# Fourth and fifth chunk of image 2 put off, and the first input sums of the next image's conv made during attention's last two units

## The chip, the core and the metric

The kernel runs on one core of a Trainium2 chip. A core has a matrix engine (TensorE, PE; PEld is its loading of weights), a vector engine (VectorE, DVE), a scalar engine (ScalarE, ACT), a third one for elementwise work (GpSimd, POOL) and queues that issue DMAs (SP and POOL among them). Engines run side by side, each in its own order, and wait for one another by semaphores. The metric is device time in microseconds (us), the median of several runs; a profile comes from one execution of its own.

## What is computed

Four images of 256 channels and 48x48 pixels go through two layers with residuals. Cut to what matters:

```python
for each layer: x = x + layer(group_norm(x))          # 32 groups

# layer 0
x = relu(batch_norm(conv3x3(x)))                      # fixed statistics
q, k, v = split(qkv_w @ x)                            # 8 heads of 32
out = v @ softmax(q.T @ k / sqrt(32)).T               # 2304 x 2304 per head
out = proj_w @ out + proj_b

# layer 1
guidance = conv3x3(x, W_cat)                          # 45 channels
outs = [x]
for i, d in enumerate((1, 6, 12, 24, 36)):
    w = softmax(guidance[:, 9*i : 9*i+9], axis=1)     # nine weights a pixel
    outs.append(sum(shift(x, dy*d, dx*d) * w[k] for k, (dy, dx) in ...))
y = W_scale @ concat(outs)                            # 1536 -> 256, a 1x1 conv
y = (y - mean(y)) / sqrt(var(y) + eps) * gamma + beta # over all four images
```

Everything is float32. The last line needs the statistics of y over all images, so nothing of the result is written before every y is known.

## The kernel before

**Stages.** The 256 channels are two halves of 128 partitions. An image's 2304 pixels are six chunks of 8 rows (384 pixels, `CH`). The stages in order: conv and q,k,v of image 0; attention 0; stage 1; attention 1; stage 2; attention 2; stage 3; attention 3; stage 4. Stage b (1 to 3) is one merged stretch: the second layer of image b-1 (`dynamic_filters`) and the conv and q,k,v of image b (`conv_blocks`) fill each other's waits. Stage 4 is the second layer of image 3 by itself, with what was put off, and then `finish`.

**Order of work.** The order on each engine is the order in which the program issues it. Within a merged stage a planner decides this: `clock` (class `Clock`) holds a modelled time for each engine, and a step adds its modelled duration. `drive(streams)` goes through a list of generators; each yields the modelled time at which its next step is due, and the first in the list that is due goes on. Where none is due, the next piece of the conv (`other`) is taken, if its own due time `need[0]` has come. `run(ns)` issues so much conv work by itself. Streams of stage b: `rest` (the conv's later input sums), `loads`, `far` (filters of dilation 6 to 36, as matmuls, in ACT and DVE copied to a tile `far`), `near` (dilation 1: nine times ACT copies a weight row `wb`, DVE multiplies it with the image into `prod`, L1792, and POOL adds `prod` into `near`, L1798), `filters` (guidance conv `pg`, softmax) and `mixes` (the 1x1 conv, `py`, chunk by chunk).

**Chunks put off.** `mixes` takes the chunks 0 to 5 in order. In stage 3 the chunks in `LATE` of image 2 aren't mixed: once their products are there, x (normalized), `near` and `far` are written to HBM, `late_d` (SP queue, L1864 and L1865: 384 KB and 1.5 MB). During attention 3 they come back, the first entry of `LATE` into the unused one of the two padded images `pads`; `late()` mixes them in stage 4 (matmuls `pl`), where they fill waits of image 3. `last_loads` loads the y of the other chunks from `y_d` in stage 4. For a chunk that is mixed, `done` copies y out of the accumulator (for chunk 5 into rows of the padded image, L1831), takes its statistics on DVE, and writes it to `y_d`.

**Memory.** Tiles are taken from pools. The pools of an attention reuse the memory of the stage before it and the other way round; the tile framework makes an instruction wait until what was there has been read or written.

**Attention.** Units 0 to 7 are 512 columns of queries for four heads (one of the halves); unit 8, `last`, is the last 256 columns of both halves. Each unit goes through 18 tiles of 128 keys, index m. `scores` makes four matmuls of 512 columns into PSUM (`so`, `se`) and two exponentials on ACT (L1330, L1331) into p, 128x2048; p has four buffers. `weigh` follows one step behind: matmuls `num` with v, and on DVE `acc` += p (L1370) for the softmax's denominator. At five values of m (`LENT`; four in the last unit) DVE adds only a quarter of p, and a DMA issued by POOL (L1372, L1374) adds the rest in memory, into a part of `ring`; at the unit's end DVE adds that to `acc`. `close(u)`, a unit or two later, sums `acc` over the partitions by matmuls (`den`, L1386), transposes, takes the reciprocal and scales the result `ao` on DVE. In the last unit the tiles m = 16 and 17 aren't added by DVE but go into `den` by matmuls, and `close` follows at once. `project` (matmuls `pp`, L1444) puts a chunk through proj_w, and DVE adds bias and residual into the padded image (L1453) and takes statistics (L655); five chunks are done at m = 6 of the units 3, 5, 7 (two) and 8, the sixth after attention. With each of the five a fifth of the next image is normalized by ACT (`spare`, `pieces`).

**The conv of images 1 to 3** (class `Blocks`) is a fast convolution with six input transforms along the rows: v1 to v4 are sums of rows of the normalized padded image d0 to d5 with factors 2 and 4, v0 and v5 likewise. They take one buffer each of 128x1200 (two halves of 600). `stage0` makes the first of them: two multiplications on ACT (L1013, L1014), ten sums on POOL (L1006); `along(i)` then takes differences along the columns (four POOL sums of 128x576, L1084), which are the moving operands of the matmuls `pc` (L1166; 128x288). `stage0` is called by `following[0]` when the last attention step has been issued, into the buffers of k and q. Tile order is v1, v2, v3, v4, v0, v5, each for two output halves `o` and four j. ACT and DVE combine the `pc` results into `one`, `two`, `held` and outputs `y`, to which ACT applies batch norm and ReLU (`relu`). `either` gives a sum to POOL or DVE by the planner's clock.

**The group norm between the layers.** `Norm.finish`: two aggregations on DVE, a matmul `pm` with the group matrix, squares on ACT, a matmul `pv`, and the reciprocal root; `shift_of` makes -mean*rstd on DVE (L685). Then DVE normalizes one half of the image and ACT the other, in two parts.

The start of a merged stage, after the last attention step:

```python
            while chunk < NCK:
                ...
                project(b, chunk, ao, pp, norm)
                chunk += 1
            table(AF.Sqrt)
            run(2400)
            for at, _ in enumerate(norm.finish(misc)):
                run((600, 700)[at])
            norm.shift_of()
```

Of the kernel before, what the change touches and what calls it, by code (L numbers as in the profile page):

```python
# [16 lines left out]
N = HH * WW  # L17
# [20 lines left out]
LATE = (5, 4)  # L38
# [19 lines left out]
def conv_preact_kernel(  # L58
# [487 lines left out]
    with tc.tile_pool(name="w", bufs=1) as wpool, tc.tile_pool(  # L546
# [98 lines left out]
        class Norm:  # L645
# [11 lines left out]
            def finish(self, psum_tile):  # L657

                mean = small.tile([P, NH], F32, tag=f"gmean{self.tag}", name=f"gmean_{self.name}", bufs=1)
                rstd = small.tile([P, NH], F32, tag=f"grstd{self.tag}", name=f"grstd_{self.name}", bufs=1)  # L660
                d2 = small.tile([P, NH], F32, tag="gd2", name=f"gd2_{self.name}")
                mv = self.mv
                for h in range(NH):
                    nc.vector.bn_aggr(mv[:, h, :], self.st[:, h].rearrange("p c s -> p (c s)"))
                yield
                pm = psum_tile(f"pm_{self.name}")
                nc.tensor.matmul(pm[:, :NH], gmat, mv[:, :, 0], start=True, stop=True)
                nc.scalar.copy(mean, pm[:, :NH])
# [82 lines left out]

        XT = WW // 2
# [222 lines left out]
        class Blocks:  # L975


            def __init__(self, b, gn):
                self.b = b
                self.d = [gn[:, :, r : r + HH - 3 : 4, :] for r in range(6)]  # L980
                k_, q, v = (
                    act.tile([P, NH * N], F32, tag=tag, name=f"cv_{b}_{tag}") for tag in "kqv"
                )
                at = NH * 2 * TJ * PADW
                v_ = [t[:, at * j : at * (j + 1)] for t in (k_, q) for j in range(3)]
                self.spare = [
                    t[:, at // 2 * j : at // 2 * j + 2 * TN]
                    for t, n in ((k_, 6), (q, 2)) for j in range(n)
                ]
                self.first = [t[:, 3 * at : 3 * at + 2 * TN] for t in (k_, q)]  # L990
                self.v = {
                    i: t.rearrange("p (h t w) -> p h t w", h=NH, w=PADW)
                    for i, t in zip((1, 2, 3, 4, 0, 5), v_)
                }
                z = 4 * NH * XN
                self.v[6] = v[:, z : z + at].rearrange("p (h t w) -> p h t w", h=NH, w=PADW)
                self.held = v.rearrange("p (j o n) -> p j o n", j=4, o=NH)
                self.of = {1: v[:, :z]}
                pad = gn.rearrange("p h r w -> p (h r w)")
                self.pad = [pad[:, z * j : z * (j + 1)] for j in range(2)]  # L1000
                self.end = {}
                self.passed = set()

# [55 lines left out]
            def axpy(self, out, x, a, y):  # L1059
                if len(x.shape) == 4:  # L1060
                    for h in range(NH):
                        self.axpy(out[:, h], x[:, h], a, y[:, h])
                    return
# [25 lines left out]
        def either(out, a, c, op, *after):  # L1089

            part = 0.5 if len(out.shape) == 2 and out.shape[-1] == XN else 1.0
# [6 lines left out]
        def conv_blocks(b, psum_tile, blocks, pool, hid):  # L1098
# [3 lines left out]
            rows = hid.rearrange("p h (t r w) -> p h t r w", r=4, w=WW)  # L1102
# [10 lines left out]
            def relus(limit):  # L1113
                while results and results[0][3] + 150 <= limit:
                    o, r, y, end = results.pop(0)
                    nc.scalar.activation(
                        rows[:, o, :, r, :], rows_of(y), AF.Relu,
# [39 lines left out]
            for t, (i, o) in enumerate(TILES):  # L1157
                u = us.pop(t)
                y = target(i, o).rearrange("p (n s) -> p n s", s=2)
                for n, j in enumerate((1, 2, 0, 3)):  # L1160
# [33 lines left out]
                    else:  # L1194
                        to = y[:, :, n - 2]
                        if busy_dve():
                            nc.scalar.mul(to, m, 1.0 if j == 0 else -1.0)
                            end = clock("ACT", 450, clock.t["PE"])
                            either(to, to, two[:, n - 2], ALU.add, end)
                        else:  # L1200
                            if j == 0:
                                tt(to, m, two[:, 0], ALU.add)
                            else:
                                tt(to, two[:, 1], m, ALU.subtract)
                            end = clock("DVE", 480, clock.t["PE"])
                        if n == 3:
                            after(i, o, y.rearrange("p n s -> p (n s)"))
# [87 lines left out]
        def attention(b, q, k_, vT, pools, spare, project, scratch, following):  # L1295
# [41 lines left out]
            def weigh(u, m, p):  # L1337
# [6 lines left out]
                several = len(units[u]) > 1  # L1344
# [68 lines left out]
            for i, (u, m) in enumerate(steps):  # L1413
# [18 lines left out]
            assert not spare  # L1432
# [30 lines left out]
        def dynamic_filters(b, ao, chunk, norm, other, pools):  # L1463
# [482 lines left out]
            def last_loads():  # L1946
# [5 lines left out]
                for c in range(NCK - len(LATE)):  # L1952
                    tag, bufs = ("prod", PRODS) if c < PRODS else ("cat1", 2)
# [34 lines left out]
            if not alone:  # L1988
                clock.t["POOL"] = clock.t["PE"] + 12500
# [12 lines left out]
            run(2400)  # L2002
            for at, _ in enumerate(norm.finish(misc)):
                run((600, 700)[at])
            norm.shift_of()
            for part in range(2):
# [9 lines left out]
                run((900, 1600)[part])  # L2016
# [7 lines left out]
            else:  # L2024
                streams.insert(0, coming[-1].rest() if coming else iter(()))
# [120 lines left out]
        for b in range(B + 1):  # L2146
# [170 lines left out]
            spare = []  # L2317
            following = [lambda: None] * 2
            clear(pads[b % 2] if b else pads[1])
            if b + 1 < B:  # L2320
# [19 lines left out]
                spare = [lambda some=todo[i::5], f=pieces: f(some) for i in range(5)]  # L2340
            norm1 = Norm("n1", b)
            q, k_, vT = qkv[b]
            with tc.tile_pool(name=f"work0_{b}", bufs=2) as work0, tc.tile_pool(
# [4 lines left out]
                    lambda c, ao, pp, b=b, n=norm1: project(b, c, ao, pp, n), scratch, following,  # L2348
                )
# [75 lines left out]
```

## Time and profile before

| what | us |
|---|---|
| runs | 2758.36, 2760.39, 2761.98; median 2760.39 |
| the profiled execution, its own time | 2758.79 |
| its span, first to last instruction | 2756.9 |
| conv and q,k,v of image 0 | 151.5 |
| attention 0, 1 | 364.70, 369.95 |
| stage 1, 2 | 294.65, 295.67 |
| stage 4 | 257.26 |

Busy over the whole span: PE 94%, DVE 76%, ACT 66%, POOL 29%; the mean granted clock of TensorE is 0.982 of full speed. The lines below name an instruction by its line (L1370), engine, operation, output and inputs. "128x2048" is partitions by elements. A number after x is a count. In brackets stands how long the engine was idle before the instruction, and what ended that. Stage borders are taken where attention's first matmuls start and where its last scores end; a few instructions of the neighbour lie on either side.

### The profile page before, as it was taken

What the parts mean: (1) busy time and instruction counts of PE and PEld (TensorE: products, weight loads), DVE (VectorE), ACT (ScalarE), POOL (GpSimd) and SP (SyncE); (2) the same over time, 40 slices, a digit from 0 to 9 for tenths busy, and PEclk for the clock granted to TensorE, in tenths of its full rate; (3) what the DMA queues carried; (4) which work ended last, traced back from release to release, by engine and by line L of the source; (5) the groups of instructions that cost most, each with busy time, mean ns of one, the idle gap of its engine ahead of it and who ended that gap; (6) DMA issues with size and microseconds to landing.
All of it is one profiled execution on the core that took longest, in us unless ns stands there. A gap on an engine that the chain in (4) does not pass through costs nothing. (4 is left out here: it accounts for less than half of the span.)

```text
span 2756.9 us, 42411 instructions
## 1 busy us (share of the span) xinstructions
PE 2602.5 (94%) x16906; PEld 1097.9 (40%) x16906; DVE 2090.5 (76%) x2030; ACT 1807.9 (66%) x2251; POOL 790.0 (29%) x871
## 2 busy tenths in 40 slices
PE   6999999999999999989999999998997999999994
PEld 5632222455552222445554222244554222235452
DVE  7778888657749888857765898884875988885476
ACT  3478988634458888844346888873344988874344
POOL 5100100466520100167560100026644000100462
PEclk9999999999999999999999999999998999999997
DMA  4704544322252444422224444442225334432365
GB/s 177 215 20 97 112 98 101 81 78 82 77 102 58 109 98 92 110 75 77 81 64 83 97 101 102 104 92 72 76 66 140 99 91 99 104 81 74 108 194 180
DMA packets 135982, 273.67 MB, mean 99 GB/s; under 512 B 56040, under 2 KB 97936, under 8 KB 134880
## 3 DMA queue, kind: packets, MB, share of 16 engines
q0 software_dynamic: 25952, 135.74, 21.5%
q1 hardware_dynamic: 109824, 135.14, 18.3%
q8 instruction: 135, 2.21, 0.3%
q14 instruction: 71, 0.58, 0.1%
HBM read 112.12 MB, written 36.04 MB: 54 GB/s over the span
## 5 line engine op out<-in xcount | busy, mean ns | idle before, releaser
L1370 DVE TENSOR_TENSOR acc<-acc,p 128x2048 f32<-128x2048 f32 (+1 forms) x568 | 1052.0, 1852 | 122.5 <-ACT p L1331 72.6
L1331 ACT ACTIVATE p<-se 128x1536 f32<-128x1536 f32 x648 | 938.6, 1449 | 0.0
L1322 PE MATMUL so<-q,k 32*128 32x512 f32 (+1 forms) x1440 | 728.2, 593 | 27.3 <-ACT p L1330 27.1
L1322 PE MATMUL se<-q,k 32*128 32x512 f32 (+1 forms) x4320 | 737.6, 593 | 4.6 <-DVE prod L1792 4.6
L1351 PE MATMUL num<-p,vT 128*32 128x512 f32 (+1 forms) x5760 | 709.1, 561 | 2.2 <-ACT ao L1380 2.2
L1330 ACT ACTIVATE p<-so 128x512 f32<-128x512 f32 x648 | 388.4, 599 | 205.6 <-PE se L1322 87.7
L1798 POOL TENSOR_TENSOR near<-near,prod 128x384 f32<-128x384 f32 x384 | 389.5, 1045 | 344.7 <-DVE prod L1792 342.9
L1322 PEld LDWEIGHTS so<-q,k 32*128 32x128 f32 x1440 | 216.7, 183 | 545.2 <-ACT p L1330 504.1
L1374 POOL DMA_DIRECT2D ring<-p x124 | 105.5, 851 | 777.9 <-ACT p L1331 464.6
L1351 PEld LDWEIGHTS num<-p,vT 128*32 128x32 f32 x5760 | 135.7, 108 | 479.1 <-issue 448.1
L1792 DVE TENSOR_TENSOR prod<-wb,pad 128x768 f32<-128x768 f32 x192 | 181.8, 953 | 102.4 <-ACT wb L1779 71.8
L1893 PE MATMUL py<-far,wsc 128*128 128x384 f32 x704 | 236.0, 488 | 0.0
L1322 PEld LDWEIGHTS se<-q,k 32*128 32x128 f32 x4320 | 227.5, 183 | 10.4 <-issue 5.5
L1779 ACT COPY wb<-ws 128x384 f32<-128x384 f32 x216 | 109.2, 509 | 147.3 <-DVE prod L1792 103.2
L1372 POOL DMA_DIRECT2D ring<-p x32 | 17.9, 559 | 610.6 <-ACT p L1331 451.3
L1494 ACT COPY far<-far 128x512 f32<-128x512 f32 x106 | 110.3, 1109 | 91.5 <-PE far L1726 91.5
L1893 PEld LDWEIGHTS py<-far,wsc 128*128 128x128 f32 x704 | 131.3, 190 | 88.7 <-issue 2.5
L1526 PE MATMUL pg<-pad,wcat 128*45 128x384 f32 x864 | 151.3, 502 | 9.4 <-ACT lg L1584 9.1
L1246 PE MATMUL pq<-hid,wqkv 128*128 128x384 f32 x384 | 132.2, 499 | 2.2 <-ACT q L1253 1.3
L1370 DVE TENSOR_TENSOR acc<-p,p 128x2048 f32<-128x2048 f32 x36 | 82.2, 2284 | 29.5 <-ACT p L1331 29.5
L1246 PEld LDWEIGHTS pq<-hid,wqkv 128*128 128x128 f32 x384 | 73.4, 194 | 53.8 <-issue 3.0
L1526 PEld LDWEIGHTS pg<-pad,wcat 128*45 128x45 f32 x864 | 54.6, 122 | 96.0 <-issue 82.4
(310 smaller groups left out, 2720.2 us busy)
## 6 DMA issues: line engine op xcount, KB each, us to landing
ring<-p POOLq DMA_DIRECT2D x156, 768.0 KB, 5.7
ws<-w_d SPq DMA_DIRECT2D x216, 192.0 KB
ring<-u_d SPq DMA_DIRECT2D x36, 512.0 KB
pad<-in_x SPq DMA_DIRECT2D x14, 1152.0 KB
xst<-in_x POOLq DMA_DIRECT2D x36, 192.0 KB, 3.7
x_d<-pad SPq DMA_DIRECT2D x36, 192.0 KB
u_d<-pad SPq DMA_DIRECT2D x12, 512.0 KB
y_d<-y SPq DMA_DIRECT2D x14, 384.0 KB
```

Source lines behind the costliest of these rows:

```text
L1246: nc.tensor.matmul(pq[:, :CH], wqkv[:, i, s, g * P : (g + 1) * P], hid[:, i, cols], start=(i == 0), stop=(i == NH - 1),)
L1322: nc.tensor.matmul(dst[:, at : at + n], k_[r, g, m * P : (m + 1) * P], q[r, g, q0 : q0 + n], start=True, stop=True,)
L1330: nc.scalar.activation(p[:, 0, :], s1, AF.Exp, scale=QS)
L1331: nc.scalar.activation(p[:, 1:, :], s3, AF.Exp, scale=QS)
L1351: nc.tensor.matmul(st["num"][r, at : at + n], vT[:, m, g * P + j * D : g * P + (j + 1) * D], p[:, j, at : at + n], start=(m == 0 and not s ...
L1370: nc.vector.tensor_tensor(st["acc"][:, js], other[:, js], p[:, js], ALU.add)
L1494: nc.scalar.copy(dst, src)
L1526: nc.tensor.matmul(pg[64 * s : 64 * s + NG, :CH], wcat[:, ii, k, :], shifted(ii, cc, k // 3 - 1, k % 3 - 1), start=(i == 0 and k == 0), st ...
L1779: nc.scalar.copy(pw[:, :CH], fetched[c, k][0])
L1792: nc.vector.tensor_tensor(prod.rearrange("p h (r w) -> p h r w", w=WW), wb, src, ALU.mult)
L1798: nc.gpsimd.tensor_tensor(cat[:, h], cat[:, h], prod[:, h], ALU.add)
L1893: nc.tensor.matmul(py[c][:, o, :CH], wsc[:, n * NH + i, o * P : (o + 1) * P], rhs, start=(n == 0 and i == 0), stop=(n == order[-1] and i = ...
```

## The change

- `LATE` goes from (5, 4) to (4, 3): of image 2 the chunks 3 and 4 are written out and mixed in stage 4, and chunk 5 is mixed in stage 3. `last_loads` loads the y of the chunks 0, 1, 2 and 5.
- `stage0` is split. `early` hands attention a table of steps, (unit from the end, m): in the last but one unit, at m = 8 to 13, ACT's multiplications for v0 and v5 (four of 128x600 in place of two of 128x1200) and four POOL sums; in the last unit, at m = 3 and 4, the two sums for v1. They are written into columns of q that no later unit reads. `opening`, called where `stage0` was, takes the tiles of k and v, makes `along(1)` and v2. v3 moves into `rest`. Buffers of the transforms and of y are laid out anew for this; y has two pieces, so its views change.
- In the last unit's steps m = 16 and 17, `weigh` issues the `den` matmuls ahead of `num`.
- `Norm.finish` also makes `less` = -mean on ACT; `shift_of` is two ACT activations in place of one DVE instruction.
- `spare`: the next image's normalization is dealt out in four parts and an empty one in place of five.
- The planner: the start of a stage runs 1000 ns of conv before `pm` and after each part of the norm's end, then 1900 and 2900; POOL's modelled time starts at PE's, no longer 12500 ns after it; `rest` is third in the list of streams, not first.

```diff
-LATE = (5, 4)
+LATE = (4, 3)
...
+                self.less = small.tile([P, NH], F32, tag=f"gless{self.tag}", name=f"gless_{self.name}", bufs=1)
...
+                nc.scalar.mul(self.less, pm[:, :NH], -1.0)
...
-                nc.vector.scalar_tensor_tensor(
-                    out=self.shift, in0=self.mean, scalar=-1.0, in1=self.rstd, op0=ALU.mult,
-                    op1=ALU.mult,
-                )
+                for h in range(NH):
+                    nc.scalar.activation(
+                        self.shift[:, h : h + 1], self.less[:, h : h + 1], AF.Identity,
+                        scale=self.rstd[:, h : h + 1],
+                    )
...
+        EARLY = 2 * TJ * PADW
...
+                self.q = qkv[b - 1][0]
...
+                    i: self.q[:, :, EARLY * j : EARLY * (j + 1)].rearrange(
+                        "p h (t w) -> p h t w", w=PADW
+                    )
+                    for j, i in enumerate((0, 5, 1))
...
+            def more(self):
+                k_, v = (
+                    act.tile([P, NH * N], F32, tag=tag, name=f"cv_{self.b}_{tag}") for tag in "kv"
+                )
+                z = 4 * NH * XN
+                at = NH * EARLY
...
+                self.of = {1: k_[:, :z]}
+                self.v.update({2: rows(k_, z), 3: rows(k_, 0), 4: rows(k_, at), 6: rows(v, z)})
+                self.spot = rows(v, 0)
...
+                self.held = v.rearrange("p (j o a n) -> p j o a n", j=4, o=NH, a=2)
...
-            def stage0(self):
+            def early(self):
...
-                nc.scalar.mul(v[0], d[2], 4.0)
-                nc.scalar.mul(v[5], d[1], 4.0)
-                self.sum(v[3], d[4], d[2], ALU.subtract)
-                self.sum(v[0], d[4], v[0], ALU.subtract)
-                self.sum(v[5], d[3], v[5], ALU.subtract)
-                self.sum(v[1], v[0], v[5], ALU.add)
+                def scale(i, h):
+                    nc.scalar.mul(v[i][:, h], d[2 if i == 0 else 1][:, h], 4.0)
+                def less(i, h):
+                    nc.gpsimd.tensor_tensor(
+                        v[i][:, h], d[4 if i == 0 else 3][:, h], v[i][:, h], ALU.subtract
+                    )
+                def both(h):
+                    nc.gpsimd.tensor_tensor(v[1][:, h], v[0][:, h], v[5][:, h], ALU.add)
+                return {
+                    (-2, 8): lambda: scale(0, 0), (-2, 9): lambda: (less(0, 0), scale(0, 1)),
+                    (-2, 10): lambda: less(0, 1), (-2, 11): lambda: scale(5, 0),
+                    (-2, 12): lambda: (less(5, 0), scale(5, 1)), (-2, 13): lambda: less(5, 1),
+                    (-1, 3): lambda: both(0), (-1, 4): lambda: both(1),
+                }
+            def opening(self):
+                v = self.v
+                self.more()
                 self.along(1)
                 self.sum(v[2], v[0], v[5], ALU.subtract)
...
-                v, d = self.v, self.d
-                nc.scalar.mul(v[6], d[3], 2.0)
-                nc.scalar.mul(v[4], d[1], 2.0)
+                d = self.d
+                nc.scalar.mul(self.v[6], d[3], 2.0)
+                nc.scalar.mul(self.spot, d[1], 2.0)
...
-                    (6, v[6], v[4], ALU.subtract), (4, v[3], v[6], ALU.subtract),
-                    (3, v[3], v[6], ALU.add),
+                    (6, v[6], self.spot, ALU.subtract), (3, d[4], d[2], ALU.subtract),
+                    (4, v[3], v[6], ALU.subtract), (3, v[3], v[6], ALU.add),
...
-        def attention(b, q, k_, vT, pools, spare, project, scratch, following):
+        def attention(b, q, k_, vT, pools, spare, project, scratch, following, early):
...
-                several = len(units[u]) > 1
+                several, end = len(units[u]) > 1, u == last
+                if end and m >= NT - 2:
+                    sums(u, p, m == NT - 2, m == NT - 1)
+                    if m == NT - 2:
+                        sums(u, st["acc"], False, False)
+                        sums(u, extra, False, False, 1)
...
-                end = u == last
...
-                    sums(u, p, m == NT - 2, m == NT - 1)
-                    if m == NT - 2:
-                        sums(u, state[u]["acc"], False, False)
-                        sums(u, extra, False, False, 1)
-                elif m == 0:
+                    return
+                if m == 0:
...
+                early.pop((u - len(units), m), lambda: None)()
...
-            assert not spare
+            assert not spare and not early
...
-                for c in range(NCK - len(LATE)):
-                    tag, bufs = ("prod", PRODS) if c < PRODS else ("cat1", 2)
+                for n, c in enumerate(c for c in range(NCK) if c not in LATE):
+                    tag, bufs = ("prod", PRODS) if n < PRODS else ("cat1", 2)
...
-                clock.t["POOL"] = clock.t["PE"] + 12500
+                clock.t["POOL"] = clock.t["PE"]
...
-            run(2400)
-            for at, _ in enumerate(norm.finish(misc)):
-                run((600, 700)[at])
+            for _ in norm.finish(misc):
+                run(1000)
...
-                run((900, 1600)[part])
+                run((1900, 2900)[part])
...
-                streams.insert(0, coming[-1].rest() if coming else iter(()))
+                streams.insert(2, coming[-1].rest() if coming else iter(()))
...
-            spare = []
+            spare, early = [], {}
...
-                    coming.append(Blocks(b + 1, pads[(b + 1) % 2]))
-                    coming[-1].stage0()
+                    coming[-1].opening()
...
+                coming.append(Blocks(b + 1, pads[(b + 1) % 2]))
+                early = coming[-1].early()
...
-                spare = [lambda some=todo[i::5], f=pieces: f(some) for i in range(5)]
+                spare = [lambda some=todo[i::4], f=pieces: f(some) for i in range(4)]
+                spare.append(lambda: None)
...
+                    early,
...
```

More of the change, by code (lines that the diff above doesn't have):

```diff
@@ L980, in __init__ @@
                 self.d = [gn[:, :, r : r + HH - 3 : 4, :] for r in range(6)]
[L981 to L990, printed above, removed]
+                self.q = qkv[b - 1][0]
                 self.v = {
-                    i: t.rearrange("p (h t w) -> p h t w", h=NH, w=PADW)
-                    for i, t in zip((1, 2, 3, 4, 0, 5), v_)
+                    i: self.q[:, :, EARLY * j : EARLY * (j + 1)].rearrange(
+                        "p h (t w) -> p h t w", w=PADW
+                    )
+                    for j, i in enumerate((0, 5, 1))
                 }
+                pad = gn.rearrange("p h r w -> p (h r w)")
                 z = 4 * NH * XN
[L996 to L999, printed above, removed]
                 self.pad = [pad[:, z * j : z * (j + 1)] for j in range(2)]
@@ L1002, in __init__, with rows, two @@
                 self.passed = set()
+            def more(self):
[4 more added lines that the diff above has]
+                at = NH * EARLY
+                def rows(t, n):
+                    return t[:, n : n + at].rearrange("p (h t w) -> p h t w", h=NH, w=PADW)
+                def two(t):
+                    return t.rearrange("p (a n) -> p a n", a=2)
+                self.of = {1: k_[:, :z]}
+                self.v.update({2: rows(k_, z), 3: rows(k_, 0), 4: rows(k_, at), 6: rows(v, z)})
+                self.spot = rows(v, 0)
+                self.first = [
+                    two(k_[:, z + at : z + at + 2 * TN]), self.q[:, :, 3 * EARLY : 3 * EARLY + TN]
+                ]
+                self.spare = [
+                    two(k_[:, n : n + 2 * TN])
+                    for n in (z, z + 2 * TN, 0, 2 * TN, at, at + 2 * TN)
+                ] + [
+                    self.q[:, :, n : n + TN] for n in (2 * EARLY, 2 * EARLY + TN)
+                ]
+                self.held = v.rearrange("p (j o a n) -> p j o a n", j=4, o=NH, a=2)
             def sum(self, out, x, y, op):
@@ L1059, in axpy @@
             def axpy(self, out, x, a, y):
[L1060 to L1063, printed above, removed]
                 nc.vector.scalar_tensor_tensor(
@@ L1089, in either @@
         def either(out, a, c, op, *after):
-            part = 0.5 if len(out.shape) == 2 and out.shape[-1] == XN else 1.0
+            part = 0.5 if out.shape[-1] in (XN, XN // 2) else 1.0
             if clock.t["POOL"] + 1300 * part <= clock.alone(*after) + 900 * part:
@@ L1101, in conv_blocks @@
             tt = nc.vector.tensor_tensor
-            rows = hid.rearrange("p h (t r w) -> p h t r w", r=4, w=WW)
+            rows = hid.rearrange("p h (a t r w) -> p h a t r w", a=2, r=4, w=WW)
             spare = list(blocks.spare)
@@ L1116, in relus @@
                     nc.scalar.activation(
-                        rows[:, o, :, r, :], rows_of(y), AF.Relu,
+                        rows[:, o, :, :, r, :],
+                        y.rearrange("p a (t w) -> p a t w", w=WW), AF.Relu,
                         bias=bn_t[:, o : o + 1], scale=bn_s12[:, o : o + 1],
@@ L1158, in conv_blocks @@
                 u = us.pop(t)
-                y = target(i, o).rearrange("p (n s) -> p n s", s=2)
+                y = target(i, o)
+                ys = y.rearrange("p a (n s) -> p a n s", s=2)
                 for n, j in enumerate((1, 2, 0, 3)):
@@ L1194, in conv_blocks @@
                     else:
-                        to = y[:, :, n - 2]
+                        to = ys[:, :, :, n - 2]
+                        halves = m.rearrange("p (a n) -> p a n", a=2)
+                        pair = two[:, n - 2].rearrange("p (a n) -> p a n", a=2)
                         if busy_dve():
-                            nc.scalar.mul(to, m, 1.0 if j == 0 else -1.0)
+                            nc.scalar.mul(to, halves, 1.0 if j == 0 else -1.0)
                             end = clock("ACT", 450, clock.t["PE"])
-                            either(to, to, two[:, n - 2], ALU.add, end)
+                            either(to, to, pair, ALU.add, end)
                         else:
                             if j == 0:
-                                tt(to, m, two[:, 0], ALU.add)
+                                tt(to, halves, pair, ALU.add)
                             else:
-                                tt(to, two[:, 1], m, ALU.subtract)
+                                tt(to, pair, halves, ALU.subtract)
                             end = clock("DVE", 480, clock.t["PE"])
                         if n == 3:
-                            after(i, o, y.rearrange("p n s -> p (n s)"))
+                            after(i, o, y)
                     free["c"].append(end)
```

## The prediction

> **What bounds the kernel now.** I first split the span into its stages (the windows view: length, busy time and instructions of PE, its weight loads, DVE, ACT and POOL, then granted clock, DMA share, GB/s). These rows are attention 2, stage 3, attention 3, and the last two units of attention 2.
>
> ```profile
> 1476.47:1845.30 368.83, 362.28 (x2964) 101.59 (x2966) 323.32 (x210) 321.84 (x343) 30.84 (x39) 1.00 0.42 93
> 1845.30:2119.96 274.66, 253.22 (x1140) 151.31 (x1141) 179.61 (x248) 119.79 (x206) 170.41 (x150) 0.95 0.30 80
> 2119.96:2499.74 379.78, 365.25 (x2962) 101.94 (x2966) 324.22 (x210) 314.58 (x330) 34.18 (x47) 0.98 0.43 100
> ...
> 1783.50:1846.30 62.80, 62.80 (x756) 27.83 (x759) 58.06 (x40) 54.92 (x59) 6.55 (x8) 1.00 0.46 97
> ```
>
> PE is busy 92 to 98% of each stage: time can be won only where PE stands still or runs at a lower clock, and in an attention whatever makes ACT or DVE late reaches PE soon. Attention 3 is 379.78 - 368.83 = 10.95 us longer than attention 2 with as many matmuls. So I read the timeline of its start (start, duration, engine, instruction, in brackets the idle time before and its releaser).
>
> ```profile
> 2114.10 1.31 PE L1322 MATMUL so<-q,k 32*128 32x512 f32 x2
> ...
> 2116.82 5.75 POOL L1798 TENSOR_TENSOR near<-near,prod 128x384 f32<-128x384 f32 x6 [0.33 <-DVE prod L1792]
> ...
> 2119.97 2.08 PE L1322 MATMUL se<-q,k 32*128 32x512 f32 x6 [4.56 <-DVE prod L1792]
> ...
> 2123.03 0.37 SPq L1865 DMA_DIRECT2D late_d<-far  x1
> ...
> 2129.95 0.60 ACT L1330 ACTIVATE p<-so 128x512 f32<-128x512 f32 x1 [11.18 <-DMA late_d<-far]
> ...
> 2130.60 1.22 PE L1322 MATMUL so<-q,k 32*128 32x512 f32 x1 [8.54 <-ACT p L1330]
> ```
>
> PE has no work: stage 3 leaves its last product and sums of the sixth chunk (DVE, POOL) and the write of that chunk's 1.5 MB to HBM to the end, and the first exponentials wait for the memory those hold. PE loses 4.56 + 8.54 = 13.1 us. The so matmuls here take 1.2 to 1.3 us against a mean of 593 ns, so the clock has dropped too.
>
> Third, the start of the next image's conv (PE, then POOL), alike in stages 1 to 3:
>
> ```profile
> 1853.32 2.82 PE L1444 MATMUL pp<-ao,wp 128*128 128x384 f32 x8 [0.39 <-DVE ao L1408]
> 1858.49 5.63 PE L1166 MATMUL pc<-cv_v,ring 128*128 128x288 f32 x14 [2.35 <-POOL cv_v L1084]
> ...
> 1868.72 1.24 PE L1166 MATMUL pc<-cv_v,ring 128*128 128x288 f32 x4 [1.51 <-ACT one L1181]
> 1871.16 0.75 PE L1166 MATMUL pc<-cv_v,ring 128*128 128x288 f32 x2 [1.20 <-DVE two L1192]
> ...
> 1849.08 5.29 POOL L1006 TENSOR_TENSOR cv_q<-pad,cv_q 128x600 f32<-128x600 f32 x4
> ```
>
> 0.39 + 2.35 + 1.51 + 1.20 = 5.45 us are idle, and 14 pc matmuls take 5.63 us (0.40 each) where six later ones take 1.70 (0.28): 14 x 0.12 = 1.7 us more from the clock.
>
> **Part 1, chunks 3 and 4 put off in place of 4 and 5.** PE's matmuls only change places. Chunk 5 is now mixed in stage 3, its last sums beside the far matmuls of the same chunk: 16 py matmuls at 488 ns and a few of the conv (8 us) cover the 6 us of POOL sums. The first exponential then waits for no write of the last chunk; chunk 4's 1.5 MB leave a chunk earlier. Gain: 13.1 us of gaps, and clock: the 15 us after 2119.96 show 6.49 us of PE work at 0.50 (3.2 lost), the 15 before 9.55 at 0.83 (1.6); as chunk 5's end will leave some hole, I count half of 4.8, 2.4. Against it +1: the last conv tile's chain (ACT 0.45, POOL 0.75 and 1.3, ACT 0.66, 3.2 us) stands right before the first q,k,v matmuls, of which the later order covers some 2. Two ACT copies of chunk 5's y (0.43 each, as at the end of stage 2) and two y writes on SP also come before attention 3's first exponentials, where ACT idled 11 us and SP's next loads (`pad<-in_x`) have a whole attention. Sum -14.5 (bounds -10, with no clock gain and 3 us of new stall, to -18).
>
> **Part 2a, what leaves the conv's start.** Two ACT multiplications of 128x1200 (1.2 us each) and eight POOL sums of 128x600 (1.36 each) go from the start, two of them (v3) behind it; four sums `along` and two for v2 stay. The first `along` can begin at the end of the last scores and takes 4 x 1.16 = 4.6 us, so the tile is ready about when den closes: 2.35 us of idle go. What is late next: the norm's sums. project on DVE takes 0.62 + 0.56 + 0.60 + 0.56, the two aggregations 0.57, 2.9 us after pp; in the new order only three pc matmuls (0.28 to 0.49 each) stand in front of `pm`, so PE waits some 1.6 there, 1.45 at the second tile (DVE's output behind a normalization of 1.76 us) and 0.7 at its next: 3.75 in place of 5.45, -1.7. No gap is long, so I let the clock stay up: -1.7. Sum -3.4 a start (bounds 0 and -7.1).
>
> **Part 2b, what enters attention's last two units.** Four ACT multiplications of 128x600 (0.6 each, half of 1.2) and six POOL sums (1.36). ACT has about 0.1 us to spare a step (2.05 of work in 2.12), so up to 2.4 us come through; but DVE is worse placed: 58.06 us busy of 62.80, its idle stretches 0.69 + 1.35 + 0.20 = 2.24 us, and its last sum `acc` ends at 1846.32, 0.6 us before PE reads it. If POOL's sums ran beside DVE's at no cost, this would be +0.5. The trace says otherwise (stage 3):
>
> ```profile
> 1905.83 1.50 POOL L1093 TENSOR_TENSOR cv_v<-cv_q,cv_v 128x576 f32<-128x576 f32 x1
> ...
> 1906.29 1.36 DVE L1095 TENSOR_TENSOR cv_k<-cv_k,two 128x288 f32<-128x288 f32 x1 [0.23 <-ACT cv_k L1197]
> ...
> 693.43 0.45 DVE L1095 TENSOR_TENSOR cv_k<-cv_k,two 128x288 f32<-128x288 f32 x1
> ```
>
> The same DVE sum takes 0.45 alone and 1.36 beside a POOL sum, and ends 0.32 after it (1907.65, 1907.33): it waited for the whole of it. Six sums cost DVE up to 6 x 1.36 = 8.2; less 2.24 idle, less 0.6 ahead of PE, less 0.6 beside transposes out of PSUM: +4.7 (bounds +0.5, all hidden, to +8.2). ACT's 2.4 run at the same time and are not added.
>
> The Trainium skill has the rule, on its page "SBUF — State Buffer", section "Who interferes with whom": a VectorE instruction with two SBUF inputs contends with a GpSimd instruction that reads SBUF, whoever is first holds the port for its whole instruction, and the other blocks. It speaks against this change: `acc` has two SBUF inputs, and so has every early sum. By the rule alone the charge would be 8.2 us in each of three attentions; by a reading that POOL is a spare engine, nothing. The row above agrees with the rule on who blocks; what the idle time absorbs is my estimate.
>
> Per transition +4.7 - 3.4 = +1.3, three times: +3.9.
>
> **Smaller parts.** The reordered den matmuls bring PE to `acc` 0.9 us earlier (8 num matmuls less before it), where it now waits 0.3: +0.3 in attention 3, within 2b in the others; their end gains nothing, since the num matmuls follow. The shift on ACT takes 0.69 us from DVE and adds two small ACT steps and one for `less` (0.2 each as the pm copy's 0.16): nothing, the normalization behind it starts as soon. In stage 4 `pm` has four matmuls in front in place of nine and waits 0.6: +0.6. New planner times and rest() third only shift where PE works; the gaps within stage 3 are some 10 us, near's chain is done earlier: -0.5 a stage, -1.5 (bounds +6 to -6).
>
> **Sum.** -14.5 + 3.9 + 0.3 + 0.6 - 1.5 = -11.2. The profiled execution (2758.79, its span 2756.9) would come to 2747.6, a span of 2745.7; the median of the runs shown, 2760.39, is 1.6 above it, so **2749.2**.
>
> **The rivals.**
> - *The early sums are hidden.* DVE's narrow steps (0.5 us where a DMA adds the rest) leave holes and POOL slips into them: +0.5 in place of +4.7, 3 x 4.2 less: 2737. For it: POOL is busy 6.55 us of the last 62.8. Against it: only 2.24 us of DVE idle.
> - *What part 1 wins part 2 gives back.* 8.2 in each attention: 3 x 3.5 more than forecast, 2760. For it: the 1.36 row.
> - *Slower: POOL's queue behind the lock.* POOL also issues the DMAs `ring<-p` that free p buffers, of which there are four. A sum that waits for DVE's 1.86 before its own 1.36 takes 3.2 us, and a DMA behind it is late by that, then ACT (it needs the buffer), then PE. Two such DMAs in units 7 and 8: 2 x 3.2 + 8.2 = 14.6 an attention, +11.2 with the start's gain, against +1.3: 3 x 9.9 = 30 above the forecast, 2779. Slower begins where a transition nets (15.1 + 5.5) / 3 = 6.9, 15.1 being what the other terms win. Against it: a DMA comes only at every third step, and each sum is issued just behind one.
> - *Part 1 doesn't remove the wait.* Chunk 5's sums still end after PE's last work, and the exponentials wait for them as for the write: 14.5 comes back, 2764. Against it: the 8 us of cover.
>
> **How the numbers follow.** A measurement of this kernel tells about 0.2% (5.5 us) from no change. Chances: forecast 0.45, hidden sums 0.20, given back 0.15, POOL's queue 0.14, no gain from part 1 0.06. Faster (under 2754.9): most of the first (0.38), all of the second, a little of the third (0.03): 0.61. Slower (over 2765.9): the fourth and 0.03 of the third and fifth: 0.17. Same: 0.22. The forecast alone spans 2742 to 2757; with the hidden sums on one side and the given-back and half of the fifth case on the other, and the bounds of the single terms, the range is 2732 to 2768.
>
> **What would show it.** Attention 3 near 371 us, its first exponential with no wait for late_d, `so` at 0.6 us at once. At the conv's start no idle before the first pc, a wait of 1 to 2 at pm. In attentions 0 to 2, den reading `acc` idle by some 4 us, and DVE sums of 3 us beside POOL's. Wrong if those sums stay at 1.85, if ACT's p waits for a buffer or `ring<-p`, or if the end of stage 3 shows a new hole of several us.

## The result, and the profile after

| | before | after |
|---|---|---|
| median of the runs | 2759.38 (2751.85 to 2761.98, 4 runs) | 2795.85 (2790.06 to 2797.67, 4 runs) |
| ratio of the times, 95% interval | | 1.0128 (1.0104 to 1.0153) |
| span of the profiled execution | 2756.9 | 2788.3 |

The kernel became 1.3% slower, where 0.4% faster was forecast. The windows view of the changed kernel, one row a stage (length; busy time and instructions of PE, weight loads, DVE, ACT, POOL; granted clock; DMA share; GB/s): attention 0, stage 1, attention 1, stage 2, attention 2, stage 3, attention 3, stage 4.

```profile
152.60:528.40 375.80, 366.50 (x2964) 102.85 (x2965) 330.23 (x210) 323.83 (x346) 42.02 (x45) 0.99 0.40 88
528.40:832.40 304.00, 281.43 (x1240) 167.68 (x1236) 183.37 (x257) 120.20 (x209) 159.14 (x147) 0.98 0.34 83
832.40:1209.80 377.40, 364.79 (x2964) 102.25 (x2966) 330.33 (x210) 323.84 (x346) 41.98 (x45) 1.00 0.40 88
1209.80:1514.10 304.30, 282.50 (x1240) 167.43 (x1239) 184.19 (x257) 120.32 (x209) 159.57 (x147) 0.97 0.33 83
1514.10:1888.90 374.80, 366.08 (x2964) 103.17 (x2966) 330.22 (x210) 323.71 (x346) 42.00 (x45) 0.99 0.40 88
1888.90:2165.80 276.90, 253.33 (x1142) 149.85 (x1140) 180.13 (x244) 116.16 (x207) 172.44 (x157) 0.96 0.32 88
2165.80:2532.70 366.90, 361.98 (x2964) 101.25 (x2964) 324.25 (x210) 314.65 (x330) 30.82 (x39) 1.00 0.43 96
2532.70:2788.30 255.60, 210.12 (x974) 114.31 (x970) 146.79 (x217) 99.28 (x150) 94.73 (x96) 0.93 0.47 144
```

Against the rows of before: attentions 0 to 2 are 11.1 + 7.5 + 6.0 = 24.6 us longer, stages 1 to 3 are 9.4 + 8.6 + 2.2 = 20.2 longer, attention 3 is 12.9 shorter, the first image 1.1 longer and stage 4 1.7 shorter: 31.3 of the 31.4 us between the two profiled executions (the medians lie 36.5 apart). DVE's busy time in an attention grew by 6.8 (323.4 to 330.2) although it has no more instructions (210).

**Attention.** Counted from the first scores of a unit to those of the next, unit 8 went from 43.2, 42.2, 42.2 us to 50.8, 48.9, 49.7 in attentions 0 to 2; unit 7 from 44.5, 44.3, 44.3 to 45.2, 45.1, 45.1; in attention 3, which carries no early work, unit 8 stays (44.1, then 43.6). The timeline of attention 1 some 9 us after unit 8's first scores (start, duration, engine, instruction, idle time before and its releaser):

```profile
1170.22 0.56 POOL L1412 DMA_DIRECT2D ring<-p  x1 [13.58 <-ACT p L1370]
1170.78 2.89 POOL L1045 TENSOR_TENSOR q<-q 128x600 f32<-128x600 f32 x2
...
1170.53 3.70 DVE L1448 TENSOR_TENSOR ao<-ao,rt 128x512 f32<-128x512 f32 x1
...
1178.13 0.69 DVE L1448 TENSOR_TENSOR ao<-ao,rt 128x512 f32<-128x512 f32 x1
...
1169.52 1.06 PE L1426 MATMUL den<-acc,ones 128*32 128x512 f32 x8 [0.56 <-DVE rt L1438]
...
1171.59 1.07 PE L1395 MATMUL num<-p,vT 128*32 128x256 f32 x16
...
1177.12 0.49 PE L1361 MATMUL se<-q,k 32*128 32x256 f32 x3 [3.83 <-DVE rt L1438]
...
1178.40 1.94 PE L1395 MATMUL num<-p,vT 128*32 128x256 f32 x16
```

The two v1 sums, meant for m = 3 and 4, run back to back as soon as the DMA of m = 2 has been issued: nothing but the queue holds POOL, and what the sums read had long been ready. DVE is in `close` there; its scaling of `ao` takes 3.70 us in place of 0.69 and ends 0.56 after the second sum. The next transpose is late, the `den` tile in PSUM is free late, the scores need its place, and PE stands 0.56 + 3.83 us. Then 16 `num` matmuls take 1.94 us where 16 before the hole took 1.07: the clock has dropped. Over the 6 us from the hole's end the granted clock is 0.72, which loses 6 x 0.28 = 1.7 us more.

**The start of the conv**, stage 3:

```profile
1896.94 2.85 PE L1485 MATMUL pp<-ao,wp 128*128 128x384 f32 x8
1899.62 1.62 PE L1203 MATMUL pc<-cv_k,ring 128*128 128x288 f32 x6
1902.60 0.38 PE L668 MATMUL pm_n<-mvn,gmat 128*128 128x2 f32 x2 [1.36 <-DVE mvn L665]
...
1904.75 5.70 PE L1203 MATMUL pc<-cv_k,ring 128*128 128x288 f32 x20
```

One hole of 1.36 us is left of 5.45, and 20 pc matmuls run at 0.28 us each. From the last scores to the first `pg` a stage takes 21.4 to 21.5 us where it took 25.6 to 26.6. The start itself won more than forecast; whether the stage did is another question (below).

**Later in the stages** new holes stand; three of stage 2 (PE), and what DVE and POOL do ahead of the second:

```profile
1275.36 1.84 PE L1567 MATMUL pg<-pad,wcat 128*45 128x384 f32 x10 [3.37 <-ACT lg L1625]
...
1347.14 0.90 PE L1687 MATMUL xa<-ident,own 128*128 128x128 f32 x3 [4.91 <-DVE own L1537]
...
1449.28 1.65 PE L1285 MATMUL pq<-hid,wqkv 128*128 128x384 f32 x2 [4.09 <-ACT hid L1151]
...
1341.00 1.44 DVE L1130 TENSOR_TENSOR cv_v<-q,cv_v 128x576 f32<-128x576 f32 x1
1341.79 4.94 POOL L1128 TENSOR_TENSOR pad<-q 128x576 f32<-128x576 f32 x3
1342.37 1.70 DVE L1099 SCALAR_TENSOR_TENSOR cv_k<-cv_v 128x576 f32<-128x576 f32 x1
1344.10 1.60 DVE L1130 TENSOR_TENSOR cv_v<-cv_v 128x576 f32<-128x576 f32 x1
1345.63 1.46 DVE L1537 COPY own<-pad 128x384 f32<-128x384 f32 x1
...
1447.57 0.76 DVE L1130 TENSOR_TENSOR q<-q,cv_v 128x576 f32<-128x576 f32 x1
```

PE waits at `xa` for a copy (`own`) that stands in DVE's queue behind sums of the conv. Those take 1.4 to 1.7 us beside POOL's sums, where one alone takes 0.76; `own` itself takes 1.46 here, and about 0.5 where no POOL sum runs. In stage 3 the holes at the first `pq` are 6.1 and 1.8 us. Before, the longest hole at `xa` in stage 2 was 1.0, at `pg` 2.2, and there was none above 0.3 at the first `pq`.

### The profile page after: what moved, and what is told of

Read it like the earlier page. It is cut to its first block, busy times and chain, and to the rows that moved or that the text cites. A ratio compares the mean times of both kernels' runs of the same rounds, so it can differ in the third digit from the quotient of the medians.

```text
span 2788.3 us, 42482 instructions
## 1 busy us (share of the span) xinstructions
PE 2614.6 (94%) x16906; PEld 1102.7 (40%) x16906; DVE 2111.1 (76%) x2031; ACT 1808.7 (65%) x2279; POOL 792.4 (28%) x869
## 3 DMA queue, kind: packets, MB, share of 16 engines
q0 software_dynamic: 25952, 135.74, 21.4%
## 5 line engine op out<-in xcount | busy, mean ns | idle before, releaser
L1410 DVE TENSOR_TENSOR acc<-acc,p 128x2048 f32<-128x2048 f32 (+1 forms) x568 | 1063.8, 1873 | 117.7 <-ACT p L1370 68.1
L1535 ACT COPY far<-far 128x512 f32<-128x512 f32 x98 | 103.0, 1109 | 95.5 <-PE far L1767 93.4
L1767 PE MATMUL far<-amat,xT 64*128 64x256 f32 x576 | 88.1, 404 | 6.0 <-DVE far L1537 5.1
```

What stands on the lines that cost most here:

```text
L1410: nc.vector.tensor_tensor(st["acc"][:, js], other[:, js], p[:, js], ALU.add)
```

## The experiments

Stage lengths are from one profiled execution each, and the executions of one kernel lie up to 0.6% apart (`late_only`: 2753.21 to 2769.96). Stages 1 and 2, which run the same program, differ by 6.3 us within the profile of `undo_rest` (below): a few us between two profiles tell nothing by themselves. Ratios are against the kernel before on the same chip.

**1. The chunks alone** (`late_only`, on the kernel before; `last_loads` takes the new list):

```diff
-LATE = (5, 4)
+LATE = (4, 3)
```

> The kernel before with the fourth and fifth chunk put off, nothing else changed. If the wait at the start of attention 3 goes with the chunks alone, attention 3 falls from 379.8 to about 367 us as it did in the changed kernel (366.9), and stages 1 and 2 stay at 294.7 and 295.7. Stage 3 then shows what the new order costs: if only the last conv tile's chain stands bare, +1 to +3 (total -10 to -12, about 2748); if the hole ahead of the first q,k,v matmuls (6.1 + 1.8 us in the changed kernel) belongs to this part, stage 3 is 8 longer and the total gains only some 5.

Measured: 2759.33 us, ratio 0.9996 (0.9976 to 1.0015): no change. Attention 3 falls from 379.8 to 369.7, but stage 3 grows from 274.7 to 283.3. Its end on PE:

```profile
2110.33 0.70 PE L1726 MATMUL far<-amat,xT 64*128 64x256 f32 x2 [2.48 <-ACT far L1494]
...
2117.12 13.20 PE L1893 MATMUL py<-far,wsc 128*128 128x384 f32 x32 [1.26 <-DVE far L1496]
2130.16 2.74 PE L1893 MATMUL py<-near,wsc 128*128 128x384 f32 x8
2135.01 0.66 PE L1322 MATMUL so<-q,k 32*128 32x512 f32 x1 [2.11 <-DVE yst L1839]
```

The write to HBM is gone from the start of attention 3, but chunk 5's mix now stands behind the last `pv`, with its own holes (2.48, 1.26, 2.11), and a hole of 3.94 has opened among the first `pq`. The wait was moved, not removed. A gain of at least 5 us was expected; none came.

**2. The planner as before** (`old_planner`) and **3. to 5. its three edits one by one**, in the changed kernel:

```diff
-                clock.t["POOL"] = clock.t["PE"]            # undo_pool
+                clock.t["POOL"] = clock.t["PE"] + 12500
-            for _ in norm.finish(misc):                    # undo_run
-                run(1000)
+            run(2400)
+            for at, _ in enumerate(norm.finish(misc)):
+                run((600, 700)[at])
-                run((1900, 2900)[part])
+                run((900, 1600)[part])
-                streams.insert(2, ...rest()...)            # undo_rest
+                streams.insert(0, ...rest()...)
```

> The changed kernel with the planner's three edits undone (conv run ahead of pm and after the norm 2400/600/700/900/1600, POOL's modelled time 12500 ns behind PE's, rest() first). Theory: stages 1 and 2 grew by 9.2 and 8.6 us because of these edits (idle 4.9 us at xa, 4.1 at the first q,k,v matmul), so both return to 290 to 295 and the kernel gains 20 to 30 us on the changed one. Rival: the early sums, which shorten the start by 4 to 5 us, leave less conv work for the holes later; then the stages stay at 302 to 306 and the time within 5 us of the changed kernel. Unit 8 of attentions 0 to 2 stays at 49 to 51 us under either.

> The changed kernel with only the amounts of conv run at a stage's start set back (2400, 600, 700, 900, 1600). old_planner, with all three planner edits set back, had its stages 1, 2, 3 at 295.7, 295.1 and 269.2 us against 304.0, 304.3 and 276.9 in the changed kernel. If these amounts decide the later holes (xa 4.9, first q,k,v matmul 4.1, pg 3.4), the stages fall to about 296, 295, 269; if the place of rest() or POOL's modelled time decides, they stay at 302 to 306 and 275 to 279.

> The changed kernel with only POOL's modelled time set 12500 ns behind PE's again. The issue order changes little by this (749 lines of PE's order differ, against some 12000 for the other two edits), so the holes should stay: stages within 3 us of 304, 304, 277. Rival: a POOL that the planner believes free too early is given sums that then stand in DVE's way, and this edit alone brings 5 us or more a stage.

> The changed kernel with only rest() first in the streams again. Its PE order is the nearest to old_planner's (4592 lines differ, 11943 against the changed kernel), so if the order of issue makes the holes, this edit brings most of it: stages at 296 to 299, 295 to 299 and 269 to 272, about 20 us in all. If the stages stay near 304 the other edits decide.

| kernel | median | ratio (95%) | stages 1, 2, 3 |
|---|---|---|---|
| changed | 2795.85 | 1.0128 (1.0104 to 1.0153) | 304.0, 304.3, 276.9 |
| old_planner | 2768.49 | 1.0024 (1.0006 to 1.0041) | 295.7, 295.1, 269.2 |
| undo_run | 2791.8 | 1.0102 (1.0046 to 1.0159) | 306.2, 306.8, 276.2 |
| undo_pool | 2791.1 | 1.0102 (1.0067 to 1.0137) | 306.5, 303.2, 275.7 |
| undo_rest | 2765.52 | 1.0008 (0.9981 to 1.0035) | 299.1, 292.8, 270.1 |

The place of `rest()` in the list of streams decides: alone it brings back 30 us (20 were expected), the other two nothing that is clear of the spread. The other runs below bear this out: in the six kernels with `rest()` third, stages 1 and 2 take 301.4 to 308.1 us (mean of the twelve 305.3), in the six with all or most of the change and `rest()` first 292.8 to 302.1 (mean 296.7). In `undo_rest` no hole above 0.9 us is left at `xa` in stages 1 and 2, and the one at `pq` is 2.48; the one at `pg` has grown to 5.29, so not every hole follows the place of `rest()`. The order on PE suggests how: with `rest` third, behind `loads` and `far`, the conv's later input sums are issued later, conv falls behind the filters and is then issued in bunches. In the changed kernel's stage 1 the last 28 pc instructions (751.0 to 761.3) have only one group of 8 `far` among them, and 8 `py` follow before the first `pq`; in `undo_rest` 44 `py` and two such groups of `far` stand among the last 24 pc. That the bunches make the holes is read from these timelines; no run isolates it.

**6. The v1 sums at m = 6, 7. one at m = 3 and one at m = 6, 8. none in attention**, in the changed kernel:

```diff
-                    (-1, 3): lambda: both(0), (-1, 4): lambda: both(1),
+                    (-1, 6): lambda: (both(0), both(1)),                     # six
+                    (-1, 3): lambda: both(0), (-1, 6): lambda: both(1),      # one_sum
```

In no_early `opening` makes all of `early`'s scalings and sums first, and attention gets none.

> The changed kernel with the two sums for v1 issued at m = 6 of the last unit (beside project, where DVE waits for pp and reads only one operand from SBUF) and not at m = 3 and 4. Theory: POOL ran both at once, right behind the DMA of m = 2, and held DVE's scaling of ao for 3.70 us in place of 0.69, which held the den tile, the scores and PE (0.56 + 3.83 us idle, then half clock). Then unit 8 falls from 50.8, 48.9, 49.7 to 42 to 44 us, L1448 back to 0.7 throughout, -20 us in all, about 2776. Rival: the four scalings on ACT, the four sums of unit 7 or the earlier den matmuls make unit 8 late; then it stays near 49 and the time within 4 us.

> The changed kernel with one of the two sums for v1 left behind the DMA of m = 2 and the other issued at m = 6. A dose of the lock: with two sums DVE's scaling of ao took 3.70 us and PE stood 3.83 + 0.56, with none 0.7 and unit 8 took 44.3. If POOL's sums hold DVE for their own length, the scaling takes 0.7 + 1.45 = 2.1 to 2.3 us with one, PE stands 1.5 to 2.8 us there, and unit 8 takes 46 to 47.5. If it isn't the sums' length but their place (any sum there upsets the close), unit 8 stays at 49 to 51.

> The changed kernel with all early scalings and sums made in opening(), after the last scores, none during attention. Theory of the lock: unit 8 at 42 to 43.5 and unit 7 at 44.3 as before; the conv's start is longer by 4 to 8 us since along(1) waits for four scalings and six sums. Net -2 to -12 against the changed kernel, and stages' later holes (pg 3.4, xa 4.9, pq 4.1) stay. Rival: the early sums cost attention nothing and unit 8 stays near 49; then the kernel is 12 to 24 us slower than the changed one.

DVE's groups by line over the last units of attention 1 (count; busy us, mean ns; idle before): the changed kernel, one_sum, six and no_early.

```profile
L1448 DVE TENSOR_TENSOR ao<-ao,rt 128x512 f32<-128x512 f32 x3 | 5.1, 1696 | 0.1
```

```profile
L1448 DVE TENSOR_TENSOR ao<-ao,rt 128x512 f32<-128x512 f32 x3 | 3.7, 1227 | 0.1
```

```profile
L1448 DVE TENSOR_TENSOR ao<-ao,rt 128x512 f32<-128x512 f32 x3 | 2.1, 692 | 0.1
```

```profile
L1449 DVE TENSOR_TENSOR ao<-ao,rt 128x512 f32<-128x512 f32 x3 | 2.1, 692 | 0.1
```

And what is left of PE's hole in six, at the same place in attention 1:

```profile
1169.50 0.49 PE L1361 MATMUL se<-q,k 32*128 32x256 f32 x3 [0.82 <-DVE rt L1438]
```

Three scalings take 5.1, 3.7, 2.1 and 2.1 us with two sums, one, none and none beside them: 1.4 to 1.6 a sum, a POOL sum's own 1.45. The one that meets them takes 3.70, 2.30 and 0.69. PE's hole in attention 0 was 3.83, 2.42 and 0.82 (two, one, none), again 1.4 and 1.6 a sum; the shorter hole ahead of it, 0.56, stays in all three. Without early work both are absent, as before the change. In six no v1 sum has run yet when these two holes come, so their 0.56 + 0.82 = 1.4 us belong to the four sums and four scalings of unit 7, which make the close late. Unit 8 took 50.8, 48.9, 49.7 (two), 49.0, 47.5, 48.8 (one), 45.8, 44.3, 44.3 (none there, two at m = 6) and 43.5, 42.2, 42.2 (none at all).

The times: six 2776.91, ratio 1.0067 (1.0045 to 1.0090), 19 us under the changed kernel as expected, though unit 8 fell only to 44.3 to 45.8 and not to 42 to 44; no_early 2773.41, 1.0040 (1.0025 to 1.0055), 22 under it, more than the 2 to 12 expected, because the start lost only 1.2 us (22.7 from the last scores to the first `pg`, against 21.5); one_sum, a single time, 2786.73.

One sum cost unit 8 more than the 46 to 47.5 expected in two attentions of three. The clock falls after the shorter hole as well: over the 6 us from its end in attention 1 it is 0.72 with one sum, as with two, and 1.00 in six. So 44.3 in six, 1.6 of hole and 1.7 of clock make 47.6 with one sum (47.5 measured), and 1.4 more make 48.9 with two (48.9). At m = 6 the same two sums meet `acc` (7.36 us for four additions against 6.28 in no_early) and DVE's wait for `pp`, which shrinks from 1.35 to 0.18 us; PE has no hole there that its waits show.

Early work was wanted for a shorter start; it buys 1.2 us there (2.0 to 2.6 with the old planner, old_planner against best) and costs 8 to 9.5 in each attention.

**9. to 12. What is left of the change**, on the changed kernel: best (no early work, all three planner edits undone), rest_no_early (no early work, only `rest()` first), rest_six (`rest()` first, v1 sums at m = 6), best_old_chunks (best with `LATE = (5, 4)`).

> The changed kernel with the three planner edits set back and all early work moved to opening(), so that neither attention's last units nor the planner carry anything of it; what is left is the put-off chunks 3 and 4, the new buffers, the sums of v3 later, the den order and the norm's shift on ACT. If the two costs are independent, attentions 0 to 2 are at 366 to 368 and the stages at 297, 296 and 270 (each start 1.2 longer than in old_planner): 2768.5 less 24 plus 4, about 2748 to 2752, 8 to 14 under the kernel before. If early sums and planner depend on each other (the stages go to 300 or more), it is no better than the kernel before.

> The changed kernel with rest() first again and all early work in opening(); the other planner edits stay. If the two costs add (undo_rest had stages 299.1, 292.8, 270.1; work in opening() takes 1.2 from each start but frees 8 to 10 in each attention), about 2765.5 - 25 + 4 = 2745, 5 to 8 under the version with all planner edits set back (2751.5). If the shorter start is what made those stages short, it ends at 2750 to 2756.

> The changed kernel with rest() first again and the v1 sums at m = 6 of the last unit: does any early work in attention pay? Units 7 and 8 took 45.1 and 44.3 with this place against 44.0 and 42.2 with none, so an attention loses 3; the start gains 1.2 (21.5 against 22.7 from the last scores to the first pg). If that is all, it is 3 x 2 = 5 us slower than rest_no_early; if the first sums' earlier end lets the later stage run ahead too, it is equal or faster.

> The version best with the chunks 4 and 5 put off as before, all else the same. In late_only the other chunks brought 10 us in attention 3 and cost 8.6 in stage 3, nothing in sum. If that holds here too, attention 3 goes from 368 to 378 to 382, stage 3 from 275.5 to 266 to 270, and the time is within 4 us of best. If the hole ahead of q,k,v came from late_only's other order and is covered here, this version is 8 to 12 us slower than best.

| kernel | median | ratio (95%) |
|---|---|---|
| best | 2751.47 | 0.9955 (0.9935 to 0.9975) |
| rest_no_early | 2746.22 | 0.9941 (0.9922 to 0.9959) |
| rest_six | 2750.05 | 0.9960 (0.9941 to 0.9979) |
| best_old_chunks | 2751.40 | 0.9965 (0.9948 to 0.9982) |

All four beat both kernels; among them the intervals overlap. The two costs add up, as expected. Early work at m = 6 (rest_six) shows no gain over none (rest_no_early). In best's profile the whole gain lies in attention 3, 368.1 us against 379.8; attentions 0 to 2 are 1.6 shorter in sum, and stages 1 to 3, whose starts are 2.4 to 2.8 us shorter each, are 3.8 longer in sum (stage 3 took 275.4 where 270 was expected). best_old_chunks was expected to have attention 3 at 378 to 382 again; it has 367.3, at a stage 3 of 276.1:

```profile
2115.04 1.95 POOL L1840 TENSOR_TENSOR near<-near,prod 128x384 f32<-128x384 f32 x2 [1.03 <-DVE prod L1834]
...
2126.42 1.12 PE L1362 MATMUL so<-q,k 32*128 32x512 f32 x2
...
2127.63 0.60 ACT L1370 ACTIVATE p<-so 128x512 f32<-128x512 f32 x1 [0.63 <-PE so L1362]
```

POOL's last sum of chunk 5 ends 9 us before attention's first scores, and the exponential waits only for those. In its order on PE the last filter matmuls stand between the q,k,v matmuls and not behind them. It pays for that with holes of 4.2 and 4.0 us at the first `pq`, where the kernel before had none. So the chunks aren't what removed the wait there either; some part of the rest of the change (v3 made later, the buffers, the order of `den`, the norm's shift on ACT) moves the conv against the filters. Which one wasn't tried, nor the changed kernel itself with the old chunks.

## Why the prediction was wrong

- **Planner**: "only shift where PE works", -0.5 a stage with bounds of 6 either way in all, is the step that failed worst: 304.0 + 304.3 + 276.9 less 295.7 + 295.1 + 269.2 = 25.2 us, and in the medians 27 (old_planner) and 30 (undo_rest). The term that decided the result was the one put near nothing, without a row that shows what the new order does.
- **Part 1, the start of attention 3**, was read rightly as a wait and put at -14.5; attention 3 fell by 12.9. That this belongs to the chunks isn't borne out: alone they bring nothing (0.9996), and with the old chunks (best_old_chunks) the wait is gone as well. The step took one hole by itself and didn't ask where the planner would put the moved mix. In the changed kernel 24 `pv` also stand behind the mix; in late_only nothing does. The +1 charged for the chain ahead of the first q,k,v matmuls was too small: the holes there are 7.9 us in the changed kernel's stage 3, 4.8 in late_only and 8.1 in best_old_chunks. That is the "new hole of several us" which the prediction had named as a sign of being wrong.
- **Part 2a**, the start: -3.4 a start forecast; in stage 3 idle fell by 4.1 and the clock stayed up (1.7), so about -5.8. Only the stall at `pm` (1.36, forecast 1.6) came; those at the second tile didn't. But no_early keeps all but 1.2 of it: the larger cut of the start comes from what isn't early, such as v3's move. And the step took a shorter start for a shorter stage. In old_planner the starts of stages 1 and 2 are 4.4 and 4.8 us shorter than before, the stages 1.0 longer and 0.6 shorter; the mean of 296.7 over twelve such stages with `rest()` first isn't below the 294.7 and 295.7 of before either. So no gain of the start shows in the length of a stage; which later wait takes it back isn't shown.
- **Part 2b**, attention: +4.7 forecast, bounds 0.5 to 8.2; measured against no_early 9.2, 9.5 and 7.9. The lock was right and the 1.36 row was the right witness, but the place and the path were wrong. The sum treated six sums as one load on DVE that shows at the last `acc`, less DVE's idle time. In fact the early work of unit 7 cost 1.0 to 1.1 there (against no_early's 44.2, 44.0, 44.0) and 1.4 in unit 8, and the two v1 sums the rest of unit 8's 6.7 to 7.5, some 5.3 to 6.1: they met one instruction, behind which hang a transpose, a PSUM place and the scores. By 1187 DVE was idle again for 2.85 us, too late for PE. The clock after the hole (1.7 us) wasn't in the sum. The forecast also took the table's m = 3 and 4 for the time when the sums run; it is only their place in POOL's order. And the 1.86 us taken for one `acc` is a mean of two shapes: 2.29 for 128x2048, 0.69 (not 0.5) for 128x512.
- **The sum**, by three ratios in a chain (each difference is good to some 8 us): from the changed kernel to old_planner 1.0128 to 1.0024, 29 us for the planner's edits in place of -1.5; from there to best 1.0024 to 0.9955, 19 us for the early work; from there to the kernel before 12 us of gain for all the rest. Early work and rest together were forecast at -9.7 and measured +7. So -11.2 + 30 + 17 makes 36, against 35 by the ratio 1.0128.
- **The rivals**: the slower one had POOL's queue and the lock, but its price hung on late `ring<-p` DMAs and buffers of p. In units 7 and 8 of attentions 0 to 2 of the changed kernel ACT's exponentials waited for scores; the only wait for a DMA is one of 1.4 us in attention 0, and the kernel before has 1.7 there. The rival's 2779 came nearest of the five, for the wrong reason.

## What to carry to other kernels

A POOL instruction put at a step in the program isn't paced by that step: it runs when its queue and its inputs allow. Before giving POOL work beside a full DVE, look for the DVE instruction that it will meet, and follow what hangs on that one's end; a place where DVE waits is the cheaper one (unit 8 was 2.1 to 2.3 us longer than without early work with the sums at m = 6, and 6.7 to 7.5 at m = 3 and 4). Where a planner orders the work, a stream's rank is an edit like any other: try it alone, compare the stages' lengths, and count a removed hole as a gain only when neither the rest of its stage nor the neighbouring one has grown by it.

## What the hardware showed that was not expected

A waiting DVE instruction wasn't let in between two POOL sums that follow each other: it took 3.70 us with two sums, 2.30 with one, 0.69 with none, and ended 0.55 to 0.56 after the last of them. The DMA that POOL issues just ahead isn't the cause: in six it stands there as well (1165.62 to 1166.18), and the scaling that starts at 1165.93 takes 0.69. The Trainium skill, on the page "SBUF — State Buffer", section "Who interferes with whom", has the lock for a whole instruction and says that who issues first decides; these runs agree on the first. On the second, DVE's instruction shows a start of 1170.53, 0.25 us before POOL's first sum at 1170.78, and still ended after both; with one sum it is the same (1167.91 and 1168.18). Whether the recorded start is the moment that counts isn't shown.

TensorE's clock fell as far after a hole of 2.42 us as after one of 3.83 (0.72 over the next 6 us) and stayed at 1.00 after one of 0.82.
